# A graph layer with masked pair sums: the degree term as a product, row matrices by per-row comparisons, comparisons moved in the step plan

## The chip, the cores and the metric

The kernel runs on one core of a Trainium2 chip. The metric is the device time of one execution in microseconds. The core has five engines with a queue each: TensorE (PE, matrix products into PSUM; its weight loads, PEld, overlap them), VectorE (DVE), ScalarE (ACT), GpSimd (POOL) and SyncE (SP, here only DMA issues). An engine works its queue in order. Engines wait for each other by semaphores, which the framework sets from the tiles that an instruction reads and writes.

## The reference, cut to what matters

```python
# layer 0: x is (128, 128, 64), adj is (128, 128, 128), H = 192
mask = (adj > 0.0)
diff = x[:, :, None, :] - x[:, None, :, :]
h = relu((x @ W1a)[:, :, None, :] + diff @ W1b + b1)
hm = einsum('bjkh,bjk->bjh', h, mask)
x = layernorm(x + hm @ W2 + mask.sum(-1)[..., None] * b2)
# layer 1
m = relu(relu(x @ V1 + c1) @ V2 + c2)
msg = relu(adj @ m)
x = layernorm(x + gru(msg, x))      # r, z, n gates; (1 - z) * n + z * x
```

With u = x (W1a + W1b) + b1 and v = -x W1b the pair term is relu(u_j + v_k). For one graph and node j the sum over the neighbours k of relu(u_j + v_k) is needed.

## The kernel before, in words

**Slots.** relu(a) is (a + |a|)/2; W2 is halved once (L113). The sum over neighbours of u + v comes from products with the mask; the sum of |u + v| is made slot by slot. The neighbours of j get ranks within each half of the nodes (L326, L329 `rankT`). `pick` (L426) compares the ranks with 1, 2, 3 and so on, 512 columns for four graphs at a time: each comparison gives a 0/1 matrix that picks for every j its neighbour of that rank. PE multiplies it with three bf16 pieces of v (L503, 12 matmuls for a slot pair, K = 64 rows for a half), onto a PSUM tile that ACT has seeded with u (L475). DVE sums the absolute values (L507). Eight ranks of each half are held so (four steps, `part`); nodes with more neighbours get extra rows, "segments" of four (two steps, `part1`), which belong to a node by the matrix `own`. `own` is made from the running sums `off` of the number of segments of each node: `side0` = (column >= sum before), `side1` (`past`) = (column >= sum with it), `own` = `side0` - `side1` (L374 to L383); `own32` is its fp32 copy (L386), `ownT` its transpose (L400).

**Padding.** A slot without a neighbour gives |u|. `base` puts min(u * (2 deg - tot), u * tot) into the row `part[no]`: ACT makes `most` = u * tot (L517), DVE the rest with one instruction of two SBUF inputs (L519). With npad = tot - deg, the number of empty slots, this row is deg * u - npad * |u|: the sum of u and the padding's correction in one. `together` (L528 to L533) adds the rows on POOL, `sums` (L546 to L549) gathers everything by products into hmT.

**Rest.** `second` (L203) is hm @ W2. The degree times b2 plus x is `residual` (L192, L196) on POOL: `b2bc` is b2 on all rows (made at L125 by a product), t3 = b2bc * deg, t4 = t3 + x; L206 adds t4. Then come a layernorm (statistics on DVE, L179 and L181; four instructions on POOL, L183 to L188), `turn`, three `message` parts, two `gates` parts, `update`, a second layernorm and the store.

**Order.** 128 graphs run in 32 groups of four. A group has 4 x 6 = 24 steps, one for each slot pair, and the whole order is written out by hand: `plan` names for each step the parts that begin there, relative to the group's own step 0 (`when`, and the `at` calls); a part that yields n goes on n steps later. Within a step come first the parts that go on, then the seed of the step after next and the slots of this step, then the parts that begin. The parts of a group spread over three groups' steps: preparation at -29 to -5, slots at 0 to 23, the tail at 24 + 5 to 24 + 28. So each block of 24 steps holds the preparation of the next group, the slots of this one and the tail of the last one. I number the steps of a block 0 to 23; what `when` has at -13 is at step 11 of the block before.

**Pools.** Slots have three PSUM tiles (`ps_g`). All other products share one pool of two (`ps_w`, bufs=2) in the order of the plan: the third product waits until the first has been read.

The fallback for dense inputs (from L624) is in the program and does not run on these inputs.

Of the kernel before, what the change touches and what calls it, by code (L numbers as in the profile page):

```python
# [8 lines left out]
F32 = mybir.dt.float32  # L9
BF16 = mybir.dt.bfloat16  # L10
I32 = mybir.dt.int32
AF = mybir.ActivationFunctionType
ALU = mybir.AluOpType
# [31 lines left out]
def adj_resnorm_kernel(  # L45
# [74 lines left out]
    b2bc = const.tile([N, F], F32, name="b2bc")  # L120
    iota = const.tile([N, N], BF16, name="iota")
    with tc.tile_pool(name="ps_c", bufs=1, space=bass.MemoryType.PSUM) as ps_c:
        b2row = row("b2row", b2, F)
        b2ps = ps_c.tile([N, F], F32, name="b2ps")
        nc.tensor.matmul(b2ps, ones, b2row, start=True, stop=True)  # L125
        nc.vector.tensor_copy(b2bc, b2ps)
        ips = ps_c.tile([N, N], F32, name="ips")
        nc.tensor.matmul(ips, ones_h, strict, start=True, stop=True)
        nc.vector.tensor_copy(iota, ips)

# [40 lines left out]
    def tail_parts(s, work, ps_w, n, store):  # L171

        name = s["name"]
# [16 lines left out]
        def residual():  # L190
            t3 = work.tile([N, n, F], F32, tag="t3", name=f"t3_{name}")
            nc.gpsimd.tensor_tensor(  # L192
                t3, b2bc.rearrange("p (o f) -> p o f", o=1).to_broadcast([N, n, F]), wide(s["deg"], n), ALU.mult
            )
            s["t4"] = work.tile([N, n, F], F32, tag="t4", name=f"t4_{name}")
            nc.gpsimd.tensor_tensor(s["t4"], t3, s["x"], ALU.add)  # L196
            yield 1

        def second():
            p = ps_w.tile([N, n, F], F32, tag="w", name=f"pw{name}")  # L200
            for i in range(n):
                for c in range(2):
                    nc.tensor.matmul(p[:, i, :], s["hmT"][:, i, c, :], w2c[:, c, :], start=c == 0, stop=c == 1)  # L203
            yield 1
            y = work.tile([N, n, F], F32, tag="y0", name=f"y0_{name}")
            nc.vector.tensor_add(y, p, s["t4"])  # L206
            s["x1"] = work.tile([N, n, F], F32, tag="x1", name=f"x1_{name}")
            layernorm(y, "0", s["x1"])
# [49 lines left out]
        def update():  # L258
# [11 lines left out]
            yield 5  # L270
# [5 lines left out]
        return [residual, second, turn, message1, message2, message3] + gs + [update]  # L276


    with ExitStack() as fast:
# [35 lines left out]
        def prep_parts(s):  # L315
# [25 lines left out]
            def counts():  # L341
                ov = prep.tile([N, G], F32, tag="ov", name=f"ov{g}")
                nc.gpsimd.tensor_scalar(ov, s["larger"], -float(W0), 0.0, ALU.add, ALU.max)
                up = prep.tile([N, G], F32, tag="up", name=f"up{g}")
                nc.gpsimd.tensor_scalar(up, ov, 1.0 / W1, (W1 - 1) / (2.0 * W1), ALU.mult, ALU.add)
                rnd = prep.tile([N, G], F32, tag="rnd", name=f"rnd{g}")
                nc.gpsimd.tensor_scalar(rnd, up, BIGR, None, ALU.add)
# [4 lines left out]
                s["tot"] = prep.tile([N, G], F32, tag="tot", name=f"tot{g}")  # L352
                nc.gpsimd.tensor_scalar(s["tot"], s["wseg"], 2.0, 2.0 * W0, ALU.mult, ALU.add)
                npad = prep.tile([N, G], F32, tag="npad", name=f"npad{g}")
                nc.gpsimd.tensor_tensor(npad, s["tot"], s["deg"], ALU.subtract)
                s["less"] = prep.tile([N, G], F32, tag="less", name=f"less{g}")
                nc.gpsimd.tensor_tensor(s["less"], s["deg"], npad, ALU.subtract)
                yield 1

            def offsets():  # L360
# [5 lines left out]
                off = prep.tile([N, 2, G], BF16, tag="off", name=f"off{g}")  # L366
                nc.scalar.copy(off, p)


                sides = []  # L370
                for c in range(2):
                    yield 1
                    t = prep.tile([N, G, N], BF16, tag=f"side{c}", name=f"side{c}_{g}")
                    nc.vector.tensor_tensor(  # L374
                        t,
                        iota.rearrange("p (o n) -> p o n", o=1).to_broadcast([N, G, N]),
                        off[:, c, :].rearrange("p (g o) -> p g o", o=1).to_broadcast([N, G, N]),
                        ALU.is_ge,
                    )
                    sides.append(t)  # L380
                s["past"] = sides[1]
                s["own"] = prep.tile([N, G, N], BF16, tag="own", name=f"own{g}")
                nc.vector.tensor_sub(s["own"], sides[0], sides[1])  # L383
                yield 1
                s["own32"] = prep.tile([N, G, N], F32, tag="own32", name=f"own32_{g}")
                nc.vector.tensor_copy(s["own32"], s["own"])  # L386

# [33 lines left out]
            def pick(t, i):  # L421
                def part():
                    name, n, src, first = ("pick1", W1, "place", W0 + 1) if t else ("pick0", W0, "rankT", 1)
                    if i == 0:
                        s[name] = prep.tile([N, n, G, N], BF16, tag=name, name=f"{name}_{g}")
                    nc.vector.tensor_scalar(s[name][:, i], s[src], float(first + i), None, ALU.is_equal)  # L426
                    yield 1

                return part
# [12 lines left out]
            def pieces():  # L442
# [16 lines left out]
                "pick0": [pick(0, i) for i in range(W0)], "pick1": [pick(1, i) for i in range(W1)],  # L459
# [52 lines left out]
        def base(s, i):  # L512

            def part():
                u = s["uv"][:, i, 0:H]
                most = main.tile([N, H], F32, tag="most", name=f"most{s['g']}")
                nc.scalar.activation(most, u, AF.Copy, scale=s["tot"][:, i : i + 1])  # L517
                yield 1
                nc.vector.scalar_tensor_tensor(  # L519
                    out=s["part", i][:, no, :], in0=u, scalar=s["less"][:, i : i + 1], in1=most, op0=ALU.mult, op1=ALU.min  # L520
                )

            return part

        def together(s, i):
            def part():
                f = s["part", i]
                nc.gpsimd.tensor_tensor(f[:, 0:2], f[:, 0:2], f[:, 2:4], ALU.add)  # L528
                nc.gpsimd.tensor_tensor(f[:, 0], f[:, 0], f[:, 4], ALU.add)  # L529
                nc.gpsimd.tensor_tensor(f[:, 0], f[:, 0], f[:, 1], ALU.add)  # L530
                yield 2
# [36 lines left out]
        def start_of(g):  # L568
# [3 lines left out]
                "masks": -29, "ranks": -22, "degrees": -17, "turned": -17, "counts": -15, "offsets": -13, "owners": -9,  # L572
                "places": -7, "pieces": -14, "values": (-23, -20, -18, -16),
                "pick0": (-19, -19, -16, -15, -15, -14, -12, -8), "pick1": (-6, -6, -5, -5),
# [14 lines left out]
        for g in range(ng):  # L589
# [3 lines left out]
            for i in range(G):  # L593
                at(g, i * S, base(s, i))
                at(g, i * S + 4, together(s, i))
                at(g, i * S + 9, sums(s, i))

            for t, f in zip((13 - per, 5, 10, 12, 14, 16, 18, 19, 22), tail_parts(s, work, ps_w, G, storer(g))):
                at(g, per + t, f)
# [24 lines left out]
    with ExitStack() as slow:  # L624
# [9 lines left out]
        with tc.If(flag > N):  # L634
            with tc.For_i(0, NB, 1) as b:
# [15 lines left out]
                s["deg"] = one.tile([N, 1], F32, name="d_deg")  # L651
                nc.vector.tensor_reduce(s["deg"], mask, AX.X, ALU.add)
# [26 lines left out]
                for c in range(2):  # L679
                    t = one.tile([HC, N], F32, tag="nd", name="d_nd")  # L680
                    nc.vector.tensor_mul(t, u[c], degb)
                    nc.vector.tensor_add(t, t, acc[c])
                    nc.vector.tensor_scalar_mul(hmT[:, 0, c, :], t, 2.0)
                s["hmT"] = hmT
                s["m1"] = one.tile([F + 1, 1, N], F32, name="d_m1")
# [47 lines left out]
```

## Time and profile before

| | |
|---|---|
| time, median of 3 runs | 1375.86 us (1374.83 to 1378.82) |
| the profiled execution | 1375.51 us, its span 1372.9 us |
| PE busy | 1216.6 us (89%) |
| DVE busy | 1167.1 us (85%) |
| ACT busy | 958.8 us (70%) |
| POOL busy | 851.4 us (62%) |
| granted PE clock, mean | 0.934 |
| DVE L507, the reductions | 768 x 949 ns |
| DVE L426, picks of rankT | 256 x 621 ns |
| DVE L426, picks of place | 128 x 296 ns |
| DVE L374, sides | 64 x 909 ns |
| DVE L519 | 128 x 609 ns |

How to read it: the span is from the first to the last instruction. Busy time counts an engine's own instructions; the end of a matmul is modelled, and an instruction's time can hold waiting for a memory port, so a "busy" DVE may stand still. The chain of work that ended last is followed back from the end of the program: at each step to what released the instruction, or to its predecessor on the engine. A piece in that chain is the time by which the end moves on, so it can be shorter than the instruction's own record, which overlaps its neighbours.

### The profile page before, as it was taken

The page shows a single profiled execution, that of the slowest core. Times are in us where ns is not written, and L with a number is a line of the kernel's source. Part 1 is how long each engine was busy: PE and PEld are TensorE (multiplying, and loading weights), DVE is VectorE, ACT ScalarE, POOL GpSimd, SP SyncE. Part 2 cuts the span into 40 slices and gives each one's busy share as a digit, 9 for nine tenths or more (in the row PEclk, how much of TensorE's full clock was granted, in tenths as well). Part 3 has the DMA queues.
Part 4 walks back from the last instruction along what each step waited for, and adds up shares of the span by engine and source line. Part 5 has one row for each costly group of instructions (what it writes and reads, how often), then busy time and mean ns, then how long its engine had stood idle before and what let it go on. Part 6 is the DMA issues. An engine that isn't in the chain of part 4 may idle for free.

```text
span 1372.9 us, 34372 instructions
## 1 busy us (share of the span) xinstructions
PE 1216.6 (89%) x13834; PEld 876.6 (64%) x13834; DVE 1167.1 (85%) x2238; ACT 958.8 (70%) x1698; POOL 851.4 (62%) x1294
## 2 busy tenths in 40 slices
PE   5899999999998988998899989889998888998874
PEld 2566676666676666666666666666676666666663
DVE  5988888898888898889898888889888899888871
ACT  3777777767776777777677767767777777777761
POOL 3557756667755667766666756666665666666662
PEclk7999999999999999999999999999999999999995
DMA  2000000000000000000000000000000000000000
GB/s 70 2 17 6 21 21 21 16 21 6 20 21 17 20 21 6 20 21 21 17 21 5 21 21 17 21 21 6 21 21 17 20 21 5 21 21 2 5 5 9
DMA packets 17612, 23.49 MB, mean 17 GB/s; under 512 B 2855, under 2 KB 11306, under 8 KB 17450
## 3 DMA queue, kind: packets, MB, share of 16 engines
q1 hardware_dynamic: 17450, 21.27, 5.0%
q8 instruction: 110, 1.80, 0.5%
q14 instruction: 52, 0.43, 0.1%
HBM read 17.06 MB, written 4.19 MB: 15 GB/s over the span
## 4 chain that ended last, share of the span: by engine, by line
PE 60%; DVE 28%; ACT 9%; issue 2%; POOL 2%; SPq 0%; DMA 0%; DVEq 0%; ACTq 0%; POOLq 0%
PE pv L503 21%; DVE part L507 12%; PE pu L436 6%; DVE pick L426 5%; PE ph L546 5%; PE pz L483 5%; ACT pv L475 4%; PE pw L203 4%; PE ph L547 4%; PE pa L235 3%; PE ph L549 3%; DVE side L374 2%; PE pg L248 2%; DVE r L450 2%; PE pn L227 2%
## 5 line engine op out<-in xcount | busy, mean ns | idle before, releaser
L507 DVE TENSOR_REDUCE part<-pv 128x192 f32<-128x768 f32 x768 | 723.8, 949 | 142.4 <-PE pv L503 73.7
L503 PE MATMUL pv<-b,pick 64*128 64x192 bf16 x9216 | 527.6, 249 | 43.7 <-ACT pv L475 43.6
L503 PEld LDWEIGHTS <-pick 64*128 64x128 bf16 x9216 | 354.5, 96 | 236.3 <-issue 214.5
L475 ACT COPY pv<-uv 128x768 f32<-128x768 f32 x512 | 410.6, 802 | 33.5 <-DVE part L507 29.1
L528 POOL TENSOR_TENSOR part<-part 128x384 f32<-128x384 f32 x128 | 129.0, 1008 | 289.2 <-DVE part L507 289.2
L475 ACT COPY pv<-us 128x768 f32<-128x768 f32 x256 | 205.9, 804 | 134.8 <-DVE part L507 134.4
L426 DVE TENSOR_SCALAR pick<-rankT 128x512 bf16<-128x512 bf16 x256 | 153.4, 621 | 0.0
L436 PE MATMUL pu<-wuv,xT 65*128 65x384 f32 x256 | 118.6, 546 | 21.1 <-ACT rank L395 17.8
L546 PE MATMUL ph<-ident,part 128*96 128x128 f32 x512 | 121.4, 322 | 1.9 <-POOL part L530 1.9
L547 PE MATMUL ph<-ownT,part 128*96 128x128 f32 x512 | 107.4, 295 | 3.2 <-POOL part L533 3.2
L529 POOL TENSOR_TENSOR part<-part 128x192 f32<-128x192 f32 x128 | 98.0, 766 | 10.0
L438 ACT COPY uv<-pu 128x384 f32<-128x384 f32 x128 | 61.1, 477 | 59.8 <-PE pu L436 59.0
L551 ACT COPY hmT<-ph 96x256 f32<-96x256 f32 x128 | 46.9, 367 | 76.9 <-PE ph L549 76.8
L533 POOL TENSOR_TENSOR part<-part 128x192 f32<-128x192 f32 x128 | 75.7, 592 | 35.3 <-DVE part L507 35.2
L549 PE MATMUL ph<-maskT,b 128*96 128x128 bf16 x768 | 91.9, 233 | 0.0
L546 PEld LDWEIGHTS ph<-ident,part 128*96 128x96 f32 x512 | 69.2, 177 | 24.2 <-issue 20.7
L519 DVE SCALAR_TENSOR_TENSOR part<-uv,less,most 128x192 f32<-128x192 f32 x128 | 78.0, 609 | 7.1 <-ACT most L517 7.1
L483 PE MATMUL pz<-uv,own 128*128 128x192 f32 x256 | 75.4, 377 | 9.2 <-DVE n L254 7.3
L530 POOL TENSOR_TENSOR part<-part 128x192 f32<-128x192 f32 x128 | 76.4, 597 | 10.0
L549 PEld LDWEIGHTS <-b 128*96 128x96 bf16 x768 | 82.1, 135 | 0.4
L547 PEld LDWEIGHTS ph<-ownT,part 128*96 128x96 f32 x512 | 78.1, 181 | 3.4 <-POOL part L533 3.4
L183 POOL TENSOR_SCALAR ve<-mv 128x4 f32<-128x4 f32 x64 | 17.6, 275 | 99.7 <-DVE mv L181 99.7
(130 smaller groups left out, 1863.9 us busy)
## 6 DMA issues: line engine op xcount, KB each, us to landing
adjT<-in_adjT_dram SPq DMA_DIRECT2D x32, 256.0 KB, 3.0
xT<-in_xT_dram SPq DMA_DIRECT2D x32, 128.0 KB, 3.2
x<-in_x_dram SPq DMA_DIRECT2D x32, 128.0 KB, 2.9
out_dram<-o SPq DMA_DIRECT2D x32, 128.0 KB, 1.7
bias<-piece SPq DMA_DIRECT2D x6, 0.5 KB, 1.6
wb<-in_w_dram SPq DMA_DIRECT2D x1, 48.0 KB, 2.2
wa<-in_w_dram SPq DMA_DIRECT2D x1, 48.0 KB
w2c<-in_w_dram SPq DMA_DIRECT2D x2, 24.0 KB, 1.7
```

The source lines that it names most:

```text
L426: nc.vector.tensor_scalar(s[name][:, i], s[src], float(first + i), None, ALU.is_equal)
L436: nc.tensor.matmul(p, s["xT"][:, i, :], wuv, start=True, stop=True)
L475: nc.scalar.copy(v, src.rearrange("p (c b h) -> p c b h", c=1, b=1).to_broadcast(list(v.shape)))
L483: nc.tensor.matmul(p, s["own32"][:, i, :], s["uv"][:, i, 0:H], start=True, stop=True)
L503: nc.tensor.matmul(v[:, h, j, :], pick[ks, a + j, i, :], s[f"b{c}"][ks, i, :], start=False, stop=c == 2, skip_group_check=True,)
L507: nc.vector.tensor_reduce(s["part1", i][:, k - no, :] if t else s["part", i][:, k, :], v.rearrange("p c b h -> p h c b"), AX.XY, ALU.add, ...
L519: nc.vector.scalar_tensor_tensor(out=s["part", i][:, no, :], in0=u, scalar=s["less"][:, i : i + 1], in1=most, op0=ALU.mult, op1=ALU.min)
L528: nc.gpsimd.tensor_tensor(f[:, 0:2], f[:, 0:2], f[:, 2:4], ALU.add)
L529: nc.gpsimd.tensor_tensor(f[:, 0], f[:, 0], f[:, 4], ALU.add)
L546: nc.tensor.matmul(p[:, c, :], s["part", i][:, 0, cs], ident, start=True, stop=False)
L547: nc.tensor.matmul(p[:, c, :], s["part1", i][:, 0, cs], s["ownT"][:, i, :], start=False, stop=False)
L549: nc.tensor.matmul(p[:, c, :], s[f"b{b}"][:, i, cs], s["maskT"][:, i, :], start=False, stop=b == 2)
```

## The change

1. **Degree terms by a small product.** The row `part[no]` becomes npad * |u| alone (ACT, function Abs with npad as scale, straight into the row); `most` and DVE's L519 go. `together` subtracts it. The degree times u and the degree times b2 both are deg * [x, 1] times constants: `wd` = [W1a + W1b; b1] W2/2 with b2 added on its last row, made once. A new part `scaled` multiplies ones with the mask (degrees on all 65 rows) and DVE multiplies xT with it (`xTd`); `second` adds a product of `xTd` with `wd`. `residual`, `t3`, `t4` and `b2bc` go; the sum of `second` is added to x.
2. **Row matrices by comparisons with scalars.** `side` and `past` are made graph by graph, 128 columns each, by a comparison with a per-row scalar (eight instructions for the two of 512 columns), and `off` is fp32.
3. **Counts.** Two of eight small POOL instructions go.
4. **Steps.** The picks of rankT stand in two blocks of four (steps 3 and 9) and those of place in one (step 19); before, they stood one or two at a time at steps 5, 8, 9, 10, 12, 16 and 18, 19. `own` moves from step 14 to 15, the degrees from 7 to 2, `update`'s POOL part from step 23 to 0, the second layernorm from step 4 to 13, b2's last piece stays at 13.

```diff
+    b2z = const.tile([F + 1, F], F32, name="b2z")
+    nc.vector.memset(b2z, 0.0)
+    nc.sync.dma_start(b2z[F : F + 1], b2.rearrange("(o n) -> o n", o=1))
...
+        for c in range(2):
+            nc.tensor.transpose(tps[:, c, :], wuv[:, c * HC : (c + 1) * HC], ident[0 : F + 1, 0 : F + 1])
+        nc.vector.tensor_copy(wuT, tps)
+        dps = ps_c.tile([F + 1, F], F32, name="dps")
+        for c in range(2):
+            nc.tensor.matmul(dps, wuT[:, c, :], w2c[:, c, :], start=c == 0, stop=c == 1)
+        nc.vector.tensor_add(wd, dps, b2z)
...
-        def residual():
...
-                    nc.tensor.matmul(p[:, i, :], s["hmT"][:, i, c, :], w2c[:, c, :], start=c == 0, stop=c == 1)
+                    nc.tensor.matmul(p[:, i, :], s["hmT"][:, i, c, :], w2c[:, c, :], start=c == 0, stop=False)
+                nc.tensor.matmul(p[:, i, :], s["xTd"][:, i, :], wd, start=False, stop=True)
...
-            nc.vector.tensor_add(y, p, s["t4"])
+            nc.vector.tensor_add(y, p, s["x"])
...
-            yield 5
+            yield 13
...
-                off = prep.tile([N, 2, G], BF16, tag="off", name=f"off{g}")
+                off = prep.tile([N, 2, G], F32, tag="off", name=f"off{g}")
                 nc.scalar.copy(off, p)
+                yield 3
...
-                    nc.vector.tensor_tensor(
-                        t,
-                        iota.rearrange("p (o n) -> p o n", o=1).to_broadcast([N, G, N]),
-                        off[:, c, :].rearrange("p (g o) -> p g o", o=1).to_broadcast([N, G, N]),
-                        ALU.is_ge,
-                    )
...
+                for i in range(G):
+                    nc.vector.tensor_scalar(side[:, i, :], iota, off[:, 0, i : i + 1], None, ALU.is_ge)
+                    nc.vector.tensor_scalar(s["past"][:, i, :], iota, off[:, 1, i : i + 1], None, ALU.is_ge)
+                nc.vector.tensor_sub(s["own"], side, s["past"])
...
+            def scaled():
+
+                p = ps_w.tile([F + 1, G, N], F32, tag="w", name=f"pe{g}")
+                nc.tensor.matmul(p, ones_h[:, 0 : F + 1], s["maskT"], start=True, stop=True)
+                yield 1
+                s["xTd"] = prep.tile([F + 1, G, N], F32, tag="xTd", name=f"xTd{g}")
+                nc.vector.tensor_mul(s["xTd"], p, s["xT"])
...
-                most = main.tile([N, H], F32, tag="most", name=f"most{s['g']}")
-                nc.scalar.activation(most, u, AF.Copy, scale=s["tot"][:, i : i + 1])
-                yield 1
-                nc.vector.scalar_tensor_tensor(
-                    out=s["part", i][:, no, :], in0=u, scalar=s["less"][:, i : i + 1], in1=most, op0=ALU.mult, op1=ALU.min
+                nc.scalar.activation(
+                    s["part", i][:, no, :], s["uv"][:, i, 0:H], AF.Abs, scale=s["npad"][:, i : i + 1]
                 )
+                yield 1
...
-                "masks": -29, "ranks": -22, "degrees": -17, "turned": -17, "counts": -15, "offsets": -13, "owners": -9,
-                "places": -7, "pieces": -14, "values": (-23, -20, -18, -16),
-                "pick0": (-19, -19, -16, -15, -15, -14, -12, -8), "pick1": (-6, -6, -5, -5),
+                "masks": -28, "ranks": -23, "degrees": -22, "turned": -16, "counts": -17, "offsets": -13, "owners": -8,
+                "places": -7, "pieces": -14, "values": (-22, -20, -18, -17), "scaled": 13,
+                "pick0": (-22, -16), "pick1": (-6,),
...
-            for t, f in zip((13 - per, 5, 10, 12, 14, 16, 18, 19, 22), tail_parts(s, work, ps_w, G, storer(g))):
+            for t, f in zip((5, 10, 12, 14, 16, 18, 19, 23), tail_parts(s, work, ps_w, G, storer(g))):
```

Each of the new blocks of picks begins one step after the step that `when` names.

## The prediction

> **What bounds the kernel now.** I read the page's busy line and its chain of work first, then one steady group cut into stages, then DVE's and POOL's timelines of the stage where PE stands.
>
> ```profile
> PE 1216.6 (89%) x13834; PEld 876.6 (64%) x13834; DVE 1167.1 (85%) x2238; ACT 958.8 (70%) x1698; POOL 851.4 (62%) x1294
> PE 60%; DVE 28%; ACT 9%; issue 2%; POOL 2%; SPq 0%; DMA 0%; DVEq 0%; ACTq 0%; POOLq 0%
> ```
>
> Two engines are nearly full, and the chain changes between them: PE holds 60% of it, DVE 28%. One group, cut where the chain changes hands (columns: stretch, its length, busy us of PE, PEld, DVE, ACT, POOL, granted clock, DMA):
>
> ```profile
> 600.30:604.50 4.20, 4.20 (x50) 2.73 (x50) 3.83 (x6) 3.83 (x7) 2.67 (x4) 1.00 0.02 4
> 604.50:609.20 4.70, 4.70 (x54) 3.69 (x53) 4.24 (x13) 3.37 (x7) 2.83 (x5) 1.00 0.00 2
> 609.20:616.40 7.20, 6.65 (x88) 4.52 (x87) 6.28 (x19) 4.69 (x9) 6.47 (x13) 1.00 0.06 20
> 616.40:627.40 11.00, 7.98 (x106) 5.85 (x104) 10.94 (x13) 6.86 (x13) 7.40 (x11) 1.00 0.01 1
> 627.40:633.40 6.00, 5.07 (x65) 3.60 (x60) 4.96 (x9) 5.81 (x11) 4.21 (x5) 1.00 0.28 89
> 633.40:640.90 7.50, 7.22 (x86) 5.22 (x85) 6.04 (x11) 5.34 (x12) 3.09 (x6) 1.00 0.01 2
> ```
>
> PE is busy 35.83 of 40.60 us. Of its 4.77 idle us, 3.02 lie in 616.4 to 627.4, where DVE is busy 10.94 of 11.00. What DVE does there, by the chain in order of time (start, us, what):
>
> ```profile
> 617.39 1.00 DVE pick L426
> 618.39 0.87 DVE r L450
> 619.25 1.73 DVE part L507 x2
> 620.99 1.69 DVE pick L426
> 622.68 1.02 DVE side L374
> 623.70 0.80 DVE part L519
> 624.49 0.87 DVE part L507
> 625.36 0.61 DVE side L374
> ```
>
> A pick takes 1.00 and 1.69 here. POOL's timeline, then one line of DVE's, say why:
>
> ```profile
> 620.89 1.64 POOL L454 TENSOR_TENSOR b<-r,b 128x768 bf16<-128x768 f32 x1
> ...
> 631.93 1.60 POOL L320 TENSOR_SCALAR maskT<-adjT 128x512 bf16<-128x512 f32 x1
> ```
>
> ```profile
> 632.57 0.48 DVE L426 TENSOR_SCALAR pick<-place 128x512 bf16<-128x512 bf16 x2
> ```
>
> The pick at 620.91 ends just after POOL's b has ended: beside a two-input POOL instruction it stands still. Beside the one-input maskT two picks took 0.48 together, unhindered.
>
> The Trainium skill ("SBUF — State Buffer", "Who interferes with whom") calls this an exclusive lock that any GpSimd instruction holds to its end. The b row agrees; the maskT row does not. By the rule the picks of `place`, which stay beside maskT, would wait up to 1.60 us a group (48 us in 30 groups) after the change too; by the row they wait for nothing, and my sum takes the row.
>
> Last, the clock, by whole groups:
>
> ```profile
> 604.20:644.80 40.60, 35.83 (x435) 25.61 (x433) 36.32 (x70) 29.90 (x54) 26.63 (x40) 1.00 0.06 18
> ...
> 685.80:726.40 40.60, 38.23 (x433) 27.96 (x431) 35.89 (x69) 29.37 (x53) 26.22 (x40) 0.92 0.06 18
> ```
>
> POOL's timeline has maskT at 97.98 and 28 groups later at 1253.24: 41.26 us a group on average, 40.56 in a group at clock 1.00. Thirty such groups carry the sum; the first and the last overlap less.
>
> **PE, added.** The fp32 products with wd: four a group. The chain has the eight like ones (L203, 16 records) at 1.94, so half: 0.97. The mask product for xTd is shaped like L326 with fewer rows out: 0.32. Together 1.29 of PE a group, with nothing beside it on PE: 35.83 becomes 37.12. A row reading PE's stops: twelve L503 matmuls count 0.67 in PE's timeline and step on by 0.60 in the chain, so each stop adds 0.07 to "busy"; with some seven of a dozen stops gone I take off 0.5: 36.6.
>
> **DVE, removed and added.** Out of the bounded stretch: L519 once (0.80), both sides (1.02 and 0.61), the two slow picks (1.00 and 1.69): 5.12. In: eight row comparisons of 128x128 bf16. None with a per-row scalar is in the trace. From below, a quarter of an unhindered pick: 0.28/4 = 0.07; from above, the 0.196 that strict_w (L91, 128x128 bf16, immediate scalar) lasts. I take 0.13, the step between the 128-wide casts of the setup (L79 at 5.75, L81 at 5.89): 1.04 a group, ends 0.56 and 1.57. In also: xTd, like rankT (L329, 0.68 with overlap, 0.60 by steps), and the second layernorm's statistics, moved here from step 4 (0.60 and 0.36, by steps 0.80). In all 2.44, so DVE needs 10.94 - 5.12 + 2.44 = 8.26 where PE needs 7.98 + 0.32 = 8.30. The two are even, and what decides is what the comparisons wait for.
>
> **The comparisons and POOL.** The layernorm of the output starts when DVE's statistics are ready at step 13, runs 0.23 + 1.04 + 0.62 + 0.75 with steps of 0.3 to 1.1 (2.7 in all), and b (1.64) is queued behind it: POOL is busy until about 4.4 us after the statistics. The comparisons come 0.87 + 0.60 + 0.87 = 2.3 us after the statistics if DVE runs without a stop, so they can meet the last 0.4 of the layernorm and all of b. Their wait is between 0 and 2.0 us; behind them on DVE stand `own`, the reduction of step 15 and, through `own`, PE's four transposes and all of PE behind those. By the b row (a wait of 1.5 in the pick's 1.77) the upper end is near; slack of one step on PE (1.5) covers about half. I take 1.0 of PE idle, ends 0 and 2.0.
>
> **What else PE waits for.** The 0.55 of 609.2 to 616.4 is the fourth u/v product behind the copy of rank (L395): its step moves, it goes. A new one comes: the two buffers of the auxiliary PSUM pool. The first u/v product now follows the degrees at step 2 and takes the buffer that rankT reads; rankT starts after the reduction of step 1, so PE waits about 0.55. The 0.93 after the stretch is DVE catching up: half stays, 0.45. The 0.28 (rows n before pz) stays. Sum of idle: 1.0 + 0.55 + 0.45 + 0.28 = 2.3.
>
> **POOL, ACT, DMA: nothing on the path.** POOL loses t3 and t4 (0.66 and 1.05) and two of the small counts; ACT's 0.45 for `most` becomes 0.45 for the padded row with another function, and the changed program holds two table loads, as before, so no switch. The picks of steps 3 and 9 find POOL between chains by the steps' order; if not, each block costs one wait of 0.8 (1.08 against 0.29, the pick beside L528). DMA issues stay at 32 loads of each kind and as many stores. The x row is kept until DVE's step 6 of the next group; its four buffers are refilled two groups later.
>
> **Ends.** Before the first slot (31 us): two transposes, a copy, two small products and an add lie in PE's 2.54 us of waiting before L436; the comparisons replace a 3.19 us `side` piece by a wait of 1.6 plus 1.0: -0.5. After the last slot PE runs at half clock: four more fp32 products, 3.43/2 = +1.7. First and last group save about 1.0 each: -2.
>
> **Sum.** 36.6 + 2.3 = 38.9 us a group; 30 x (41.26 - 38.9) = 71 less, and 0.8 less at the ends. The profiled execution took 1375.5 (span 1372.9 and 2.6 around it), 0.4 below the median of 1375.9, which I leave out: 1375.5 - 71.6 = **1304**.
>
> **Rivals.**
> 1. The comparisons find the port free, and the catching up goes too: 36.6 + 0.55 + 0.28 = 37.4, 30 x 3.83 = 115 less: 1260. For it: the instructions of POOL behind b wait for a later reduction, so a late DVE meets an empty POOL. Against: b itself is not late enough.
> 2. The change does not do what it says: the full 2.0 at the comparisons, and both blocks of picks meet two-input POOL work as well (1.6, half of it covered): 38.9 + 1.0 + 0.8 = 40.7, 17 less: 1358. For it: POOL's busy time falls only by some 2.2 of 26.7 us a group, so most places on DVE still lie beside POOL work.
> 3. Slower: the clock. Half-clock stretches follow the poorly filled stretch; the mean of 30 groups is 0.949, that is 4.2 us of half clock a group. Today most of it hides in PE's idle time (41.05 against 40.56 in a group at 0.92). With PE continuous it is paid in full, half of its length: with 4.2 us, 41.0 and 1368; with the 6.6 us of the rows at 0.92, 42.2 and 1403. From 4.7 us of half clock a group the change loses. Against it: PE would fill about 8.3 of 9.3 us in that stretch, not 8 of 11.
>
> The skill's "TensorE: Matmul & The Clock Gate" ("HAM oscillation — how this bites in real kernels") names idle gaps above some 3.4 us as the cause. No single gap here is that long, yet the clock drops; by the rule rival 3 would cost nothing before or after.
>
> **Numbers.** Forecast 0.47, rival 1 0.24, rival 2 0.16, rival 3 0.13 (0.10 of it slower, 0.03 no change). The range takes in rival 1 with the cheap end of the comparisons and rival 2: 1250 to 1360. Within 0.3% (4 us, about what a measurement of this kernel can tell from no change): 0.03; faster 0.87; slower 0.10.
>
> **What would show it.** Right: picks at about 0.28 in the blocks of steps 3, 9 and 19; comparisons 0.1 to 0.2 each with one long one beside POOL's b; DVE near 31 to 32 us a group; PE's share of the chain above 75%; clock above 0.95. Wrong: many comparisons above 0.5, `own` still ahead of PE's transposes with more than 1.5 us a group, a clock at or below 0.93, or a PE that waits at a new place.

## The result, and the profile after

The changed kernel takes 1392.76 us (median of 4 runs, 1385.55 to 1402.85) where the kernel before, run beside it, takes 1375.34 (1373.32 to 1378.82): a ratio of 1.0133, 95% interval 1.0097 to 1.0169. It is 1.3% slower, a small loss, but every run of it lies above every run of the kernel before; the forecast of 1304 was wrong in sign, and its range was missed. The profiled execution took 1402.85 us, the longest of the four, with a span of 1400.9 and a mean granted clock of 0.943.

The busy line and the chain of work of the changed kernel:

```profile
PE 1257.4 (90%) x14126; PEld 898.6 (64%) x14126; DVE 1073.3 (77%) x2336; ACT 959.3 (68%) x1698; POOL 782.0 (56%) x1166
PE 55%; DVE 32%; ACT 8%; issue 3%; POOL 1%; DMA 0%; SPq 0%; DVEq 0%; POOLq 0%; ACTq 0%
```

DVE and POOL lost work as meant, 94 and 69 us; PE gained 41. Yet DVE's share of the chain grew from 28% to 32%. Less work, and more of the end is made by it. The stages of one group say where (same columns as before):

```profile
602.70:616.50 13.80, 13.80 (x146) 9.45 (x145) 9.24 (x16) 9.58 (x19) 5.80 (x8) 0.83 0.01 2
616.50:628.60 12.10, 11.49 (x125) 8.13 (x124) 8.34 (x23) 6.96 (x13) 6.16 (x11) 1.00 0.01 2
628.60:637.10 8.50, 8.20 (x106) 5.75 (x105) 7.79 (x19) 8.34 (x15) 6.21 (x13) 1.00 0.00 0
637.10:645.00 7.90, 5.39 (x70) 4.32 (x70) 7.87 (x16) 4.25 (x9) 5.24 (x7) 0.99 0.27 85
645.00:646.00 1.00, 1.00 (x13) 0.79 (x12) 0.10 (x1) 1.00 (x3) 1.00 (x2) 0.50 0.00 0
```

In the stage from 637.10 to 645.00 DVE is busy 7.87 of 7.90 us and PE 5.39; right behind it the granted clock is 0.50 (half clock). The first row stands at the same place behind the group before, and its clock is 0.83 on average. DVE's timeline of the stage from 637.10, and POOL's:

```profile
638.60 0.54 DVE L374 TENSOR_SCALAR side<-iota,off 128x128 bf16<-128x128 bf16 x1
639.06 1.68 DVE L375 TENSOR_SCALAR past<-iota,off 128x128 bf16<-128x128 bf16 x1
640.66 0.24 DVE L374 TENSOR_SCALAR side<-iota,off 128x128 bf16<-128x128 bf16 x1
...
641.75 0.43 DVE L376 TENSOR_TENSOR own<-side,past 128x512 bf16<-128x512 bf16 x1
```

```profile
638.48 0.61 POOL L198 TENSOR_TENSOR o<-yc,rs 128x256 f32<-128x256 f32 x1
639.05 1.64 POOL L456 TENSOR_TENSOR b<-r,b 128x768 bf16<-128x768 f32 x1
```

The first comparison ends just after `o` does, the second just after `b`; the other six step on by 0.16. By the starts, 0.46 and 1.60 where 0.16 would do: the wait is 1.74 us. PE's waits over the whole run (us in total, times, longest):

```profile
PE pq L401 <- DVE own L376: 41.6, 30, 6.8
PE ps L410 <- ACT cat L239: 38.1, 29, 1.3
PE pu L438 <- DVE rankT L331: 19.7, 32, 0.7
```

And whole groups (from one maskT to the next), at full clock and with one and two half-clock stretches:

```profile
985.43:1026.22 40.79, 37.13 (x442) 26.66 (x442) 33.62 (x72) 29.79 (x54) 24.45 (x37) 1.00 0.06 18
560.73:602.83 42.10, 38.67 (x443) 27.58 (x439) 33.34 (x72) 29.66 (x54) 24.36 (x38) 0.95 0.06 17
602.83:646.08 43.25, 39.83 (x449) 28.39 (x447) 33.33 (x72) 30.13 (x54) 24.35 (x37) 0.93 0.05 17
```

From the maskT at 94.24 to the one 28 groups later at 1278.61 a group lasts 42.3 us; it was 41.26. At full clock 40.79 stands against 40.56 before: the work saved on DVE bought nothing there. The half clock comes on top, in both kernels: 42.3 - 40.79 = 1.5 us a group now, 41.26 - 40.56 = 0.7 before. So of the 1.04 us that a group got longer, 0.8 is clock.

### The profile page after: what moved, and what is told of

It is laid out like the page before. It is cut to its first block, busy times and chain, and to the rows that moved or that the text cites. A ratio compares the mean times of both kernels' runs of the same rounds, so it can differ in the third digit from the quotient of the medians.

```text
span 1400.9 us, 35109 instructions
## 1 busy us (share of the span) xinstructions
PE 1257.4 (90%) x14126; PEld 898.6 (64%) x14126; DVE 1073.3 (77%) x2336; ACT 959.3 (68%) x1698; POOL 782.0 (56%) x1166
## 4 chain that ended last, share of the span: by engine, by line
PE 55%; DVE 32%; ACT 8%; issue 3%; POOL 1%; DMA 0%; SPq 0%; DVEq 0%; POOLq 0%; ACTq 0%
PE pv L505 20%; DVE part L509 15%; PE pu L438 8%; PE pg L250 5%; PE pw L204 5%; PE pz L485 4%; DVE past L375 4%; ACT pv L477 4%; PE ph L545 3%; DVE pick L429 3%; DVE side L374 2%; DVE r L452 2%; PE pw L205 2%; PE ph L546 2%; ACT b L449 2%
## 5 line engine op out<-in xcount | busy, mean ns | idle before, releaser
L532 POOL TENSOR_TENSOR part<-part 128x192 f32<-128x192 f32 x128 | 75.5, 590 | 70.3 <-DVE part L509 70.3
L545 PE MATMUL ph<-ident,part 128*96 128x128 f32 x512 | 111.3, 300 | 2.0 <-POOL part L529 1.8
L529 POOL TENSOR_TENSOR part<-part 128x192 f32<-128x192 f32 x128 | 94.8, 741 | 10.0
L546 PE MATMUL ph<-ownT,part 128*96 128x128 f32 x512 | 98.6, 275 | 0.1
L548 PE MATMUL ph<-maskT,b 128*96 128x128 bf16 x768 | 85.2, 220 | 0.0
L250 PE MATMUL pg<-wcat,cat 128*128 128x256 f32 x256 | 85.1, 466 | 0.1
L204 PE MATMUL pw<-w2c,hmT 96*128 96x64 f32 x512 | 81.4, 282 | 0.0
L528 POOL TENSOR_TENSOR part<-part 128x192 f32<-128x192 f32 x128 | 75.6, 591 | 10.0
L193 POOL TENSOR_SCALAR ve<-mv 128x4 f32<-128x4 f32 x64 | 14.4, 226 | 117.8 <-DVE mv L191 117.8
L545 PEld LDWEIGHTS ph<-ident,part 128*96 128x96 f32 x512 | 63.6, 164 | 22.9 <-issue 20.7
L548 PEld LDWEIGHTS <-b 128*96 128x96 bf16 x768 | 74.4, 124 | 0.0
L375 DVE TENSOR_SCALAR past<-iota,off 128x128 bf16<-128x128 bf16 x128 | 73.1, 571 | 0.0
```

What stands on the lines that cost most here:

```text
L250: nc.tensor.matmul(p[:, i, :], s["cat"][:, i0 + i, :], wcat, start=False, stop=i == m - 1)
L375: nc.vector.tensor_scalar(s["past"][:, i, :], iota, off[:, 1, i : i + 1], None, ALU.is_ge)
L545: nc.tensor.matmul(p[:, c, :], s["part", i][:, 0, cs], ident, start=True, stop=False)
L546: nc.tensor.matmul(p[:, c, :], s["part1", i][:, 0, cs], s["ownT"][:, i, :], start=False, stop=False)
L548: nc.tensor.matmul(p[:, c, :], s[f"b{b}"][:, i, cs], s["maskT"][:, i, :], start=False, stop=b == 2)
```

## The experiments

Two theories at first. **P**: the comparisons stand behind POOL's `o` and `b`; PE idles for it and then runs at half clock for a while. **W**: PE's added work and the new turns of the two-buffer pool are what is lost. The times of the kernel before differ a little from one set of runs to the next (medians 1368.5 to 1375.3), so a difference between two versions taken in different sets is good to some 7 us; the ratios are to the kernel before in the same set. "Group" is from maskT to maskT, in a group at clock 1.00 if nothing else is said.

**1. The layernorm early again** (on the changed kernel; it lands on step 5, since `update`'s POOL part stands one step later than in the kernel before, where the layernorm was at step 4; some expectations below still call it step 4).

```diff
-            yield 13
+            yield 5
```

> The second layernorm goes back from step 13 to step 5 of the block, nothing else differs from the changed kernel; so the last piece b can run before the comparisons. Theory P (the comparisons stand behind POOL's layernorm and b for 1.9 us, PE then idles for most of one clock window and pays half clock after it): the long comparison of 1.7 goes to 0.24, groups at full clock fall from 40.8 to about 39, half-clock stretches vanish in most groups, 1270 to 1310 us. Theory W (what is lost is PE's added work and the new waits on the two-buffer pool, and the comparisons' wait is hidden): 1375 to 1400.

Measured: 1281.29 us, ratio 0.9365 (0.9302 to 0.9429), clock 0.99. One number moved back takes 111 us. The comparisons are 0.24 to 0.25 each, PE's waits for `own` and `cat` are gone, and each group is the same:

```profile
590.88:629.18 38.30, 37.05 (x443) 26.66 (x442) 31.90 (x73) 29.71 (x54) 24.42 (x38) 1.00 0.06 19
629.18:667.48 38.30, 37.05 (x443) 26.66 (x442) 31.90 (x73) 29.71 (x54) 24.43 (x38) 1.00 0.06 19
```

So the later layernorm costs 40.79 - 38.30 = 2.5 us a group without the clock, and 4.0 with it (42.3 - 38.3). This run moves the whole layernorm, its statistics on DVE too; how much of the 2.5 is the comparisons' wait, experiments 3 and 7 tell in part.

**2. PE kept busy** (six constant products, not used, written ahead of `pa` in the changed kernel).

```diff
             p = ps_w.tile([F, n, N], F32, tag="w", name=f"pa{name}")
+            for _ in range(6 if n == G else 0):
+                nc.tensor.matmul(p, ones_h[:, 0:F], strict_w..., start=True, stop=True)
```

> The changed kernel with six products of constants (128 to 64 rows, 512 columns, 0.22 us each) put ahead of the third message's product at step 16, where PE then waits for own; their result is overwritten. No wait is taken away, PE is only busy where it was idle. Theory P with the clock as its second half: no half-clock stretches, groups near the 40.8 of full clock, 1340 to 1360 us although PE does 1.3 us more a group. If the half clock is only an accompaniment that costs nothing: 1390 or more. Theory W: slower by up to 1.3 a group, 1390 to 1435.

Measured: 1357.08 us, ratio 0.9903 (0.9866 to 0.9939), clock 0.99. PE does 1.2 us more in each group and the kernel is 36 us faster:

```profile
583.47:624.27 40.80, 38.34 (x448) 27.32 (x448) 33.63 (x73) 29.81 (x54) 24.48 (x38) 1.00 0.06 18
```

The group is the 40.8 of the changed kernel at full clock, now in every group: this run prices the clock alone. The wait behind `o` and `b` is untouched by it.

**3. The comparisons in their old, wide form** at the new step.

```diff
-                for i in range(G):
-                    nc.vector.tensor_scalar(side[:, i, :], iota, off[:, 0, i : i + 1], None, ALU.is_ge)
-                    nc.vector.tensor_scalar(s["past"][:, i, :], iota, off[:, 1, i : i + 1], None, ALU.is_ge)
+                for c in range(2):
...
+                    nc.vector.tensor_tensor(t, iota..., off[:, c, :]..., ALU.is_ge)
```

> The changed kernel with the two comparisons of 512 columns against a broadcast operand (0.61 each when unhindered) in place of the eight of 128 columns (0.16 each, 1.3 together), at the same step. The form itself then saves nothing (1.2 against 1.3). Theory P: they meet the same two POOL instructions, so within 1% of the changed kernel, 1380 to 1405. If the form were a part of the loss (more instructions, more grants of the port): 1360 or less.

Measured: 1311.49 us, ratio 0.9594 (0.9529 to 0.966). I was wrong: the form matters where the port is disputed. DVE's timeline, then POOL's:

```profile
637.22 1.28 DVE L373 TENSOR_TENSOR side<-iota,off 128x512 bf16<-128x512 bf16 x2
638.53 0.72 DVE L382 TENSOR_TENSOR own<-side,side 128x512 bf16<-128x512 bf16 x1
```

```profile
637.10 1.87 POOL L198 TENSOR_TENSOR o<-yc,rs 128x256 f32<-128x256 f32 x1
638.93 1.82 POOL L462 TENSOR_TENSOR b<-r,b 128x768 bf16<-128x768 f32 x1
```

Here POOL's `o` is the one that waits (1.87, elsewhere 0.61), and `b` starts only after both comparisons. In the changed kernel `o` runs unhindered, `b` starts just as the first short comparison ends, and the second one waits for all of it. The Trainium skill ("SBUF — State Buffer", "Who interferes with whom") says that whoever issues first holds the port pair for the whole instruction. The starts in the two traces don't show that for `o`: it begins 0.12 us ahead of the first comparison in both (637.10 and 637.22 here, 638.48 and 638.60 above), and waits only here. Why is open. The two forms differ in length and in the kind of instruction (TENSOR_SCALAR and TENSOR_TENSOR), and no run takes these apart.

The group, with the layernorm still at step 13:

```profile
604.30:643.75 39.45, 37.06 (x443) 26.66 (x442) 32.86 (x67) 29.88 (x54) 25.96 (x38) 1.00 0.06 18
```

So 40.79 - 39.45 = 1.3 of the 2.5 us go with the comparisons' wait, and 1.2 stay with the later layernorm although the comparisons don't wait.

**4. The degree product alone** (parts 1 and 3 of the change on the kernel before, mask product at step 13; comparisons, picks and plan as before).

```diff
-                "pick0": (-19, -19, -16, -15, -15, -14, -12, -8), "pick1": (-6, -6, -5, -5),
+                "pick0": (-19, -19, -16, -15, -15, -14, -12, -8), "pick1": (-6, -6, -5, -5), "scaled": 13,
```

> The kernel before with the degree product and the shorter counts alone: its comparisons and its step plan stay. PE does 1.29 us a group more; DVE loses L519 and gains xTd; POOL loses t3 and t4, beside which a side and L519 stood still. Theory P: the order was the fault, so this part alone gains, about 38.5 to 40 a group, 1290 to 1340 us. Theory W: PE's 1.29 a group is paid, 1390 to 1415.

Measured: 1397.09 us, ratio 1.0217 (1.0148 to 1.0287). By itself this part loses 2.2%, some 30 us (20 to 39 by the interval), as W said. The mask product takes a turn in the two-buffer pool, and the sums of a later step now wait:

```profile
PE ph L550 <- ACT m L232: 48.8, 30, 1.6
```

**5. The order of experiment 1 without the degree product** (`most`, L519, t3, t4 and b2bc back).

```diff
-                nc.tensor.matmul(p[:, i, :], s["xTd"][:, i, :], wd, start=False, stop=True)
-            nc.vector.tensor_add(y, p, s["x"])
+            nc.vector.tensor_add(y, p, s["t4"])
...
-                    s["part", i][:, no, :], s["uv"][:, i, 0:H], AF.Abs, scale=s["npad"][:, i : i + 1]
+                nc.scalar.activation(most, u, AF.Copy, scale=s["tot"][:, i : i + 1])
+                yield 1
+                nc.vector.scalar_tensor_tensor(
```

> The layernorm at step 4, the short comparisons and the picks in blocks, but the old degree path (most, L519, t3, t4, b2bc) in place of the products. Theory A (the degree product is paid in full by PE once PE has hardly any idle time): PE 37.05 becomes 35.8 us a group, PE's waits of 0.85 stay, the group goes from 38.30 to 37.0 to 37.4, the time to 1240 to 1255. Theory B (the product pays for itself: t3 and t4 on POOL and L519 on DVE bring the stalls back, the comparisons meeting t3 or t4): group 38.3 or longer, time 1281 or more, DVE above 33.5 us a group.

Measured: 1362.37 us, ratio 0.9942 (0.9912 to 0.9972). As theory B said: the same product that lost 30 us in the old order gains 81 in this one. L519 (L514 in this kernel) is now 747 ns on average, 609 before; it stands beside `ua` and `b`. Every other group has half clock, which is about half of the 81; at full clock the group is 39.58 against 38.30:

```profile
591.08:630.66 39.58, 35.63 (x432) 25.45 (x432) 33.53 (x75) 29.44 (x53) 25.93 (x40) 1.00 0.08 22
630.66:673.01 42.35, 39.19 (x434) 28.36 (x434) 34.17 (x76) 30.24 (x55) 25.97 (x40) 0.92 0.05 14
```

**6. The order of experiment 1 with the wide comparisons** (the edits of 1 and 3 together).

```diff
-            yield 13
+            yield 5
...
+                    nc.vector.tensor_tensor(t, iota..., off[:, c, :]..., ALU.is_ge)
```

> The layernorm at step 4, the two 512-column comparisons in place of the eight short ones. Theory A (the form is worth nothing where the port is free: 8 x 0.16 against 2 x 0.64): group 38.3, time within 4 us of 1281. Theory B (the long form is dearer also alone, since it takes 0.9 with two SBUF inputs): group 0.3 or more longer, 1290 or more.

Measured: 1280.7 us, ratio 0.9356 (0.9303 to 0.941), group 38.22. Equal to experiment 1: where nothing disputes the port, eight steps of 0.16 are the same as two of 0.64, and part 2 of the change is worth nothing there.

**7. `b` later** (the changed kernel, b2's last piece at step 17 instead of 13).

```diff
                 nc.scalar.copy(s["b1"], r)
-                yield 1
+                yield 5
```

> The changed kernel with its layernorm at step 13, but with b2's last piece on POOL four steps later (step 17). Theory P (b's 1.64 us in front of the comparisons is what is paid): only o's 0.5 is left of the wait, own is 1.2 to 1.6 us earlier, the group at full clock 39.2 to 39.6 in place of 40.8, clock 0.98 or more, time 1300 to 1325. Theory W (moving the layernorm's own work, its statistics on DVE and four POOL instructions, is what is paid): little of b's wait comes back, time 1350 or more.

Measured: 1325.31 us, ratio 0.9692 (0.9631 to 0.9752), clock 0.991, group 39.86, just beyond the far end of P: 0.9 of the 2.5 us come back, and no group has half clock. PE still waits 1.1 us a group for `cat` and 0.7 for `n` (0.24 in experiment 1); the 1.6 us that remain are not in `b`. How they split between `o` and the statistics that the layernorm put ahead on DVE, I did not separate here. Experiment 3 says that most of it is not the comparisons' wait: without any such wait it kept 1.2.

**8. The product of places one step later** (the changed kernel; `places` at -6 and its picks at -5).

```diff
-                "places": -7, ... "pick1": (-6,),
+                "places": -6, ... "pick1": (-5,),
```

> The changed kernel with the product of places one step later (18) and the picks of place one step later (20), so that PE doesn't stand at it for ACT's copy of cat. Theory P (DVE's lateness behind the comparisons is the root, the wait for cat is the same lateness seen a second time): the 1.3 us wait goes or moves to the next slots, the group at full clock stays 40.5 to 40.8; time 1370 to 1393. Theory W (the wait for cat is a price of its own, of the two-buffer pool): 1.3 us a group less at full clock and less half clock, time 1320 to 1355.

Measured: 1359.21 us, ratio 0.9926 (0.9898 to 0.9954); between the two expectations. A group is 40.20 at full clock, and only about every other one has half clock (41.5). PE's wait for `cat` is gone, the one for `own` stays, and half of what is saved comes back at the next slots:

```profile
PE pq L401 <- DVE own L376: 42.0, 31, 6.8
PE pv L505 <- ACT pv L477: 32.8, 65, 1.5
```

So the wait for `cat` is for the most part DVE's lateness met a second time: 0.6 of its 1.3 us is a price of its own.

**9. Two turns freed** (on experiment 1: the first u/v product and the first product with own32 each one step later).

```diff
-"values": (-22, -20, -18, -17)
+"values": (-21, -20, -18, -17)
-            for i, t in enumerate((-4, -2, -1, 0)):
+            for i, t in enumerate((-3, -2, -1, 0)):
```

> The kernel with the layernorm at step 4, with the first u/v product one step later (step 3) and the first product with own32 one step later, so that neither takes a turn of the two-buffer pool whose tile DVE has not read yet. Theory A (PE is the bound, at 37.05 of 38.30 us a group, and its two small waits, 0.62 and 0.23, are paid in full): group 37.4 to 37.7, time 1256 to 1264. Theory B (DVE is close behind and the slot steps take the waits over): group 37.9 to 38.3, time 1270 to 1281.

Measured: 1245.45 us, ratio 0.9055 (0.9039 to 0.9071), better than I expected and the fastest version of this study. PE is the bound:

```profile
574.58:611.66 37.08, 36.59 (x443) 26.58 (x442) 31.87 (x73) 29.80 (x54) 24.41 (x37) 1.00 0.06 19
```

**10. The blocks of picks alone** (on the kernel before).

```diff
-                "pick0": (-19, -19, -16, -15, -15, -14, -12, -8), "pick1": (-6, -6, -5, -5),
+                "pick0": (-22, -16), "pick1": (-6,),
```

> The kernel before with its picks in the three blocks (steps 3, 9 and 19) and nothing else changed. Theory P (what holds the kernel before is DVE's stalls beside POOL's two-input instructions, the two slow picks of 1.00 and 1.69 with them): DVE loses 2.1 us in the bounded stretch and 1.3 or more elsewhere, picks 0.28 each, PE's idle time falls by 1.0 to 2.1, group at full clock 38.5 to 39.6, time 1290 to 1335. Theory W (the stalls move to the wide comparisons and L519, which then stand beside b): time 1350 to 1375.

Measured: 1318.92 us, ratio 0.9589 (0.9572 to 0.9606), group 39.33 (40.57 before). Theory P held. The picks are 286 ns, and one of the two wide comparisons now takes the place of the pick beside `b` (1.81 us in a steady group, 0.68 for the other); a wide comparison can stand still too:

```profile
L374 DVE TENSOR_TENSOR side<-iota,off 128x512 bf16<-128x512 bf16 x64 | 79.7, 1247 | 1.0 <-ACT off L367 1.0
```

**11. The later layernorm alone** (on the kernel before, `yield 14`, which puts it at step 13).

```diff
-            yield 5
+            yield 14
```

> The kernel before with the second layernorm at step 13 in place of step 4 and nothing else changed. Theory P (the layernorm's POOL work meets the comparisons wherever both stand at steps 13 and 14): the wide comparisons get longer (above 1.1 each on average), PE waits longer for own, group 0.5 to 1.5 longer, time 1385 to 1420. Theory W (in the kernel before DVE is stalled there already, so nothing is added): 1365 to 1380.

Measured: 1331.36 us, ratio 0.9686 (0.9657 to 0.9716). Both theories missed: the move that ruins the changed kernel makes the kernel before 44 us faster. DVE's groups of it:

```profile
L386 DVE CAST own<-own 128x512 f32<-128x512 bf16 x32 | 46.5, 1455 | 0.0
L374 DVE TENSOR_TENSOR side<-iota,off 128x512 bf16<-128x512 bf16 x64 | 45.3, 709 | 0.8 <-ACT off L367 0.8
```

The sides fell from 909 to 709 ns. There, they follow the statistics directly (step 13 and 14, no xTd between), while POOL is at the layernorm's first instructions; `b` is held back behind the layernorm, and own32 waits for it instead, 1455 ns. PE needs own32 only steps later. The meeting is the same; who is met is another. The sides are the smaller part of what DVE saves: the picks of rankT fell from 621 to 396 ns on average (the one that took 1.69 us beside `b` takes 0.28, as `b` comes later) and L519 from 609 to 421. How the 44 us split was not run apart.

**12. The comparisons at once** (the changed kernel, layernorm still at step 13, comparisons at step 13 instead of 15).

```diff
                 nc.scalar.copy(off, p)
-                yield 3
+                yield 1
```

> The changed kernel, its layernorm still at step 13, with the comparisons two steps earlier (step 13), directly behind the layernorm's statistics on DVE, so that they run while POOL is still at the layernorm's first two instructions, and b stands behind the layernorm. Theory P (the loss is the meeting of the comparisons with o and b, not the layernorm's new place): comparisons 0.25 each, own some 5 us ahead of PE's transposes; the port wait moves to own32 or xTd, for which PE does not stand waiting; group 38.3 to 39.3, clock 0.98 or more, time 1281 to 1312. Theory Q (whatever DVE instruction stands beside o and b pays the same): group 40 or more, 1340 or more.

Measured: 1412.38 us, ratio 1.0298 (1.0249 to 1.0348). The comparisons are free of POOL (281 and 251 ns on average), as P said, and the time is the worst of all, as it did not. In the trace xTd now stands on DVE behind the comparisons, `own`, a reduction and own32, and the sums' product waits for the turn that xTd reads:

```profile
PE ph L545 <- DVE xTd L387: 70.0, 30, 2.6
```

2.33 us of PE in a steady group, in one piece, and a mean clock of 0.936.

**13. Experiment 9 without the degree product** (the edit of 5).

```diff
...
-            nc.vector.tensor_add(y, p, s["x"])
+            nc.vector.tensor_add(y, p, s["t4"])
```

> The kernel with the layernorm at step 4 and the two turns freed (PE full, 37.09 us a group), with the old degree path in place of the products. Theory A (once PE is full, the product's 1.29 on PE is paid in full): group 36.0 to 36.8, time 1212 to 1238. Theory B (L519, t3 and t4 bring back stalls worth more than PE's 1.29): group 37.1 or longer, or half clock again, time 1246 or more.

Measured: 1299.43 us, ratio 0.9464 (0.9422 to 0.9507), 54 us slower than with the product. PE has 1 us less to do and still loses:

```profile
562.80:601.58 38.78, 35.65 (x433) 25.73 (x433) 33.77 (x75) 29.86 (x54) 25.76 (x40) 1.00 0.06 18
640.37:680.03 39.66, 37.43 (x434) 27.21 (x434) 34.19 (x76) 30.33 (x55) 25.81 (x41) 0.96 0.05 16
```

PE idles 3.1 us of 38.78 here (0.5 of 37.08 with the product); DVE has 1.9 us more.

**14. Experiment 12 with the mask product two steps earlier**, so that xTd is ahead of the comparisons.

```diff
-"values": (-22, -20, -18, -17), "scaled": 13,
+"values": (-22, -20, -18, -17), "scaled": 11,
```

> The changed kernel with the layernorm still at step 13, the comparisons directly behind its statistics (step 13), and the mask product with xTd two steps earlier (steps 11 and 12), so that xTd is ahead of the comparisons on DVE and the turn of the two-buffer pool that the sums of step 15 need is free. Theory P (the layernorm's place costs nothing by itself; what costs is DVE work that PE waits for and that stands behind POOL's o and b or behind the comparisons): comparisons 0.25, PE's wait for xTd and for own gone, group 38.2 to 39.0, clock 0.98 or more, time 1278 to 1305. Theory Q (statistics, layernorm and comparisons together in one place are too much for DVE there): group 39.5 or more, time 1320 or more.

Measured: 1347.48 us, ratio 0.984 (0.9785 to 0.9896), in the range of theory Q. PE's waits for xTd and `own` are gone, as P said, and the one for `cat` ahead of the places nearly so; the mask product's new place makes two others:

```profile
PE pm L222 <- ACT off L366: 21.6, 30, 0.7
PE po L363 <- ACT cat L218: 13.3, 30, 0.5
```

These are 0.72 and 0.44 a group. Added to the 38.30 of experiment 1 they give 39.5, and most of the groups without half clock measure 39.2 to 39.8. By this sum little is left at full clock for the layernorm's place itself, once nothing that PE waits for stands behind its `o` and `b`; it is a sum of waits, and no run shows it directly. About every fourth group has half clock (42.2), for a reason that I did not find.

## Why the prediction was wrong, point by point

The step that failed is "The comparisons and POOL": 1.0 us of PE idle a group, where the runs show 2.5 behind the layernorm's new place, 1.3 of it by the comparisons' wait and 1.2 without a term in the sum. With it failed the balance before it, DVE 8.26 against PE 8.30 in that stretch: DVE stayed the bound there (7.87 of 7.90 us, PE 5.39). The half clock, which the sum had at nothing, then added 1.5.

- **PE added, right; its stops, wrong for this kernel.** 35.83 + 1.29 = 37.12 was expected, and the group at full clock has 37.13. I took off 0.5 for stops that would go. They did not go here; in experiment 9, where they do, PE counts 36.59. (+0.5 a group)
- **Comparisons, right in size.** 0.16 a step, 1.3 for eight: taken 1.04, within 0.56 to 1.57. The long ones stood where I said, beside `o` and `b`.
- **Picks, right.** 285 ns in the blocks. Experiment 10 shows that this alone carried most of the forecast gain: 56 us.
- **rankT's turn, right.** 0.55 expected, 0.62 measured.
- **The comparisons' wait: this step failed.** I had put the wait between 0 and 2.0 and "slack of one step on PE (1.5) covers about half. I take 1.0 of PE idle". The wait was 1.74, in the range, but the slack did not cover it: `own` reached PE 1.20 us late in a steady group, and the ACT queue made PE late again, since `cat` stands behind a seed that waits for DVE's reduction, and the product of places needs the turn that `cat` reads: 1.31. This second wait stands nowhere in the sum. PE's idle in that place was 2.5, beyond my end of 2.0. About 1.3 of it goes with the comparisons' wait (experiment 3), which is within my ends; the other 1.2 came with the layernorm in other ways, for which the sum had nothing, and their split stays open. Idle time came to 40.79 - 37.13 = 3.7 against the 2.3 that I summed. (+1.4)
- **The clock, priced under the wrong condition.** Rival 3 said that half clock would be paid once PE is continuous, and that PE's better filling spoke against it. The runs show the reverse: in experiments 1, 2, 3, 6, 7 and 9, where PE idles 0.5 to 2.8 us a group, the clock is 0.987 to 0.991; behind the poorly filled stage (5.39 of 7.90) it drops. I had that stage filled 8.3 of 9.3. The sum of idle time alone does not tell it: experiment 10 idles 3.5 us a group with a clock of 0.981, the changed kernel 3.7 with 0.943. Its price of half the length is high: the group with a mean clock of 0.93 has some 6 us of half clock, and two stretches of it add 43.25 - 40.79 = 2.46 us, and PE's busy time 2.7. (+1.5 on the mean of the groups; experiment 2 takes it out for 36 us.) Rival 3's dearer end, a group of 42.2 and 1403, meets the measured group and the profiled execution by luck: it was 38.9 and 3.3 for the half clock, and the runs have 40.8 and 1.5.

38.9 + 0.5 + 1.4 + 1.5 = 42.3, the group measured; 30 groups of 1.04 more than before make 31, and the two profiled executions differ by 27; the rest lies at the ends. The medians differ by only 17, as the profiled execution is the longest of its four.

- **Rival 1 was a version away.** Its group of 37.4 and 1260 needed the port free; experiment 1 has it free at 38.30 and 1281, experiment 9 also without the turn of rankT at 37.09 and 1245.
- **Rival 2** had the right wait (2.0 in full), but let the group stay below the old one at 40.7; that the group at full clock was 40.79 is luck in part, since its 0.8 for the blocks of picks did not come (285 ns there), and the second wait and PE's stops stood in its place. What it lacked is the clock.
- **The signs.** Of those I named for "wrong", one is there as named, the new place where PE waits (`cat`, 1.31). The late `own` (1.20 a group) stays below my 1.5, the clock (0.943 in the profiled execution, 0.95 in the others) above my 0.93, and comparisons above 0.5 are two of eight, not many. Of those for "right", the picks came, and a long comparison beside `b`; PE's share of the chain is 55% and not above 75%. DVE is at 33.6 us a group instead of 31 to 32, the wait of 1.7 being counted as busy.
- **The degree product was priced by its instructions only.** 1.29 of PE against 0.80 of DVE looked like a loss worth taking for the stretch that DVE bounds. Its worth depends on the order: 30 us lost alone (experiment 4), 81 and 54 gained in the later orders (5 against 1, 13 against 9). It takes t3, t4 and four two-input instructions of DVE out of the dispute; that this is why is read from L519's 747 ns and DVE's 1.9 us more a group, and was not run apart.

What stays open: the remaining 1.6 us of experiment 7 (1.2 in experiment 3), what decides who waits at the port, the half clock in some groups of experiment 14, and the exact filling below which the clock drops. That xTd's turn is the cause in experiment 12 is shown by experiment 14, which takes it away; that the mask product's turn is the cause in experiment 4 is read from its trace and was not run apart.

## What to carry to other kernels

A wait for the shared port is not worth its own length but what the bounding engine gets late through it: with the comparisons' 1.7 us, 1.3 of full-clock time and the half clock's 1.5 went (experiment 3). Before moving a POOL chain, write down for both queues who will stand beside whom, and keep next to the long two-input POOL instruction only DVE work that nobody waits for (own32 in experiment 11). Try the parts of a change alone and in the final order: here one part changed sign (+30, then -54), and one number of the plan decided between 1393 and 1281.

## What the runs showed of the hardware that I had not expected

- **The form of a DVE instruction matters beside POOL.** Eight comparisons of 128 columns and two of 512 make the same group where they wait for nothing (experiments 1 and 6, 38.30 and 38.22), but beside POOL's `o` and `b` it is 40.79 against 39.45: between two short ones `b` got in. That long ones keep the port is no rule: alone a wide one takes 0.68, but beside t3 in the kernel before it took 1.10, and in experiment 10 one that met `b` under way took 1.81.
- **Half clock without a long gap.** The Trainium skill ("TensorE: Matmul & The Clock Gate", "HAM oscillation — how this bites in real kernels") names idle gaps above some 3.4 us. In the steady groups of the changed kernel no wait of PE is longer than 1.31 us, and the clock still falls to 0.83 in the stage after the one where PE is busy 5.39 of 7.90 us. That section's rule, taken alone, does not cover what several short waits in one stretch did here; 1.2 us more of PE work in that stretch keeps the clock at 0.99 (experiment 2).
- **More work on PE made the changed kernel faster**, by 36 us, with products that nobody reads (experiment 2).
